# A two-layer graph-and-transformer kernel: five edits around the score table of the first layer

## The chip, the core and the metric

The kernel is one program on one core of a Trainium2 chip. The metric is the time of one execution in device microseconds, and the time of a kernel is the median of its runs. One more execution was taken with the profiler on; its times are those of the trace.

## What is computed

The reference takes 625 nodes with 1024 features and 10,000 directed edges. Layer 0 adds graph attention, linear attention and a ternary-weight feed-forward to the nodes; layer 1 adds a neighbour-mean network, a second linear attention and a mixture of experts. The part that the change touches is the graph attention of layer 0 and what runs beside it:

```python
msg = xl[src] + xr[dst]                       # per edge, 4 heads of 64
act = jnp.where(msg > 0, msg, 0.2 * msg)
e = jnp.einsum('ehd,hd->eh', act, att)        # one score per edge and head
alpha = softmax of e over the edges of one dst (self loops included)
out = segment_sum(alpha[..., None] * xl[src], dst) @ W_up
# beside it, from the same normed x:
k, v = phi(x @ W_k + b_k), x @ W_v + b_v      # 1024 columns, made in two halves of 512
# then, node by node:
x = x + graph part + mix part + b_o
x = x + ffn(layernorm(x));  xn1 = layernorm(x)   # quantised activations, ternary weights
```

## The kernel before, in words

Nodes lie in `NT = 5` tiles of `P = 125`. All weights are float32; a weight half of 1024 x 512 is loaded by `Half` as two transfers of 1 MB on SP's queue into a pool of six buffers with the tag "w".

**The order.** In this part the order of the work on each engine is the order in which the program emits it. `Stream` (called `do`) holds back the steps that follow a matmul group, so that a group's evacuation is emitted after the next call's preparation and before the next call's matmuls; an argument-less `do()` only lets held steps out. Each engine runs its own list in order.

**The edges.** `left_right` (L537) writes the left and right projections of each tile to DRAM, `xl_d` on ACT's queue and `xr_d` on POOL's. Then POOL issues, for each of 79 chunks of 128 edges, two gathers (L601, `ga` and `gb`) and one scatter (L619) of the finished scores into `table`, a DRAM array of 625 x 625 x 4 scores that a single transfer (L395) fills with zeros first. Between them DVE adds and reduces (`score_group`, L609 to L584) and ACT raises to e (L588). A scatter waits until the scatter before it has landed. `one_beat` issues one step of this chain; `work(us)` paces the beats by the matmul time that was emitted. Five of the beats also run `self_loops(t)`: the scores of the nodes' own loops, `own`, which ACT's queue stores onto the diagonal of `table` (L164 and L165 inside `rows_dma`, two transfers for one tile: partitions 0 to 111 and 112 to 124).

**The dense work beside it.** `lin.key(t)` and `lin.value(t)` make the keys and values of one half of the columns for all five tiles, with `count()` between them (edge counts, L458); `lin.half(1)` then loads the biases (`bk_t`, `bv_t`) and the two weight halves of the second half. Queries, answers and the output projection `mixed` follow.

**The table.** After the last scatter, `load_table(t)` brings the 125 destination columns of tile t, 5 x 500 values per partition, into `tb` by two transfers on POOL's queue. `weigh(t)` multiplies them by the edge counts, one DVE instruction (L828) for each of five source tiles s; `sums(t)` contracts the result (`pg`, head by head, over all s).

**The tile periods.** A loop over `p` staggers the five tiles. In period p: `sums(p)`, `turn_sums(p)`, `weigh(p + 1)`, `up_again(p)` (L891, its evacuation into x is L896) for the graph part, and for tile p - 1 the feed-forward made by `ffn`: `p1` (layernorm and quantise, DVE), `f1` (eight transposes `ptr`, L948, evacuated at L949), `f2` (`pgu`, then a tanh on ACT and a chain on DVE), `f3` (transposes `phT`, evacuated at L980), `f4` (`pdn`, added into x at L996). For tile p - 2: `p5` (layernorm, DVE) and `f5` (eight transposes L1011, copied to `xnT1` by ACT at L1012). A `spacer` is one key or value group of layer 1's linear attention, placed between these steps. The output bias is added to x by ten DVE instructions (L1068), two for each tile: tiles 0 and 1 in period 0, tiles 2, 3 and 4 in period 1. Narrow PSUM tiles (`ps1`) take turns in two banks, wide ones (`ps2`) in three double banks.

Of the kernel before, what the change touches and what calls it, by code (L numbers as in the profile page):

```python
# [14 lines left out]
ALU = mybir.AluOpType  # L15
# [5 lines left out]
NT = 5  # L21
P = 125
# [31 lines left out]
def attempt(ctx: ExitStack, tc: tile.TileContext, w: dict, out: bass.AP, shifted: bool):  # L54

    nc = tc.nc
# [85 lines left out]
    def nodes(t):  # L142
        return slice(t * P, (t + 1) * P)
# [18 lines left out]
    def rows_dma(eng, dst, src):  # L162

        eng.dma_start(out=dst[0:112], in_=src[0:112])  # L164
        eng.dma_start(out=dst[112:P], in_=src[112:P])  # L165
# [32 lines left out]
    wpool = graph.enter_context(tc.tile_pool(name="w", bufs=6))  # L198
# [9 lines left out]
    hold = {}  # L208
# [138 lines left out]
    with ExitStack() as st0:  # L347
# [5 lines left out]
        tview = table[0:N * N, :].rearrange("(u p d) h -> p u (d h)", u=NT, p=P)  # L353
        xnT = bigT("xnT")

        with ExitStack() as edges:
# [22 lines left out]
            def load_edges():  # L379
                for dst, name in ((si, "src"), (di, "dst")):  # L380
# [10 lines left out]
            lin = LinearAttention(xnT, ("L0_Wq", "L0_Wk", "L0_bk", "L0_Wv", "L0_bv"), w["L0_bq"],  # L391
                                  lambda us: work(us), nc.sync)
# [3 lines left out]
                              in_=none.unsqueeze(1).to_broadcast([128, 28, 440]))  # L396
# [177 lines left out]
            def score(dst, m, n, p):  # L574

                by_att = att[0:p].unsqueeze(1).to_broadcast([p, n, 256])
                if shifted:
                    nc.vector.scalar_tensor_tensor(m, m, 0.2, m, op0=ALU.mult, op1=ALU.max)
                    nc.vector.tensor_tensor(m, m, by_att, op=ALU.mult)
                else:  # L580
                    nc.vector.scalar_tensor_tensor(m, m, 0.0, by_att, op0=ALU.max, op1=ALU.mult)
                nc.vector.tensor_reduce(dst, m.rearrange("p t (h e) -> p t h e", h=4), AX.X, ALU.add)
                if not shifted:
                    nc.vector.tensor_scalar(dst, dst, LIMIT, None, op0=ALU.min)  # L584

            def exp(e):
                if not shifted:
                    nc.scalar.activation(e, e, AF.Exp)  # L588
# [35 lines left out]
            own = pool.tile([P, NT, 4], FP, name="own")  # L624
# [8 lines left out]
            diagonal = table[0:N * (N + 1), :].rearrange("(s d) h -> s d h", d=N + 1)[:, 0, :]  # L633

            def self_loops(t):


                m = pool.tile([P, 1, 256], FP, tag="xd", name="gs", bufs=1)
                nc.vector.tensor_tensor(m[:, 0, :], xlr[:, t, 0:256], xlr[:, t, 256:512], op=ALU.add)
                score(own[:, t:t + 1, :], m, 1, P)  # L640
                exp(own[:, t:t + 1, :])
                rows = xlr[:, t, 0:256].rearrange("p (h e) -> p h e", h=4)
                if shifted:
                    nc.vector.tensor_copy(xl1[:, t, :, 0:64], rows)
                else:
                    nc.vector.tensor_tensor(m[:, 0, :], xlr[:, t, 0:256], att[:P], op=ALU.mult)
                    nc.vector.tensor_reduce(linear[:, t, :], m.rearrange("p t (h e) -> p (t h) e", h=4), AX.X, ALU.add)
                    part4 = pool.tile([P, 4, 1], FP, tag="part4", name="part4", bufs=2)
                    nc.vector.tensor_scalar(part4[:, :, 0], linear[:, t, :], -4.0 * LINEAR, 4.0 * LINEAR,
                                            op0=ALU.max, op1=ALU.min)  # L650
                    nc.scalar.activation(xl1[:, t, :, 64:65], part4, AF.Exp, scale=0.25)
                    nc.vector.tensor_tensor(xl1[:, t, :, 0:64], rows,
                                            xl1[:, t, :, 64:65].to_broadcast([P, 4, 64]), op=ALU.mult)
                rows_dma(nc.scalar, diagonal[nodes(t), :], own[:, t, :])

# [32 lines left out]
            def work(us):  # L690
                beat["us"] += us

                while beat["us"] >= 2.0 + 5.2 * min(beat["g"], 6) + 8.1 * max(beat["g"] - 6, 0) and chunks:
                    one_beat()
# [2 lines left out]
            states = []  # L697
            for c in range(2):
                if c:
                    lin.half(c)  # L700
                for t in range(NT):
                    for f in (lin.key, lin.value):
                        f(t)
                        part["held"] = max(part["held"] - 1, 0)
                        for _ in range(6):
                            if count():
                                work(0.7)
                states.append(lin.states())
                if c == 0:
                    for f in states[0]:  # L710
                        f()
# [15 lines left out]
            def mixed(t, ks=range(KC), keep=None, then=None, paced=True, cs=(0, 1)):  # L727
                for c in cs:
                    def pe(c=c):
                        if c == 0 and ks[0] == 0:  # L730
                            hold["px", t] = ps2("px1")
                        for k in ks:
                            nc.tensor.matmul(hold["px", t][:P, c, :], lhsT=oT[:, k, nodes(t)], rhs=wo[c](k),  # L733
                                             start=(k == 0), stop=(k == KC - 1 and keep is not None))

                    def after():
                        px = hold.pop(("px", t))
                        for c in range(2):
                            nc.vector.tensor_tensor(keep[:, c, :], px[:P, c, :], bo[c][:P], op=ALU.add)  # L739

                    do(None, pe, after if keep is not None and c == 1 else None)
                    if then is not None and c == 0:
                        then()
                    if paced:
                        work(0.87 * len(ks))
# [29 lines left out]
            for m in range(KC):  # L775
# [5 lines left out]
                if m < 3:  # L781
# [3 lines left out]
                                      in_=w[("w_gate", "w_up", "w_down")[m]].rearrange("(k p) n -> p k n", p=128))  # L785
# [4 lines left out]
            bo = [lin.bias(w["L0_bo"], c, tag) for c, tag in enumerate(("bk_t", "bv_t"))]  # L790
# [4 lines left out]
            kept = mid([P, 2, 512], "kept")  # L795
# [14 lines left out]
        x = xpool.tile([P, NT, D], FP, name="x")  # L810
# [3 lines left out]
        def load_table(t):  # L814

            hold["tb", t] = mid([P, NT, P, 4], "tb")
            if not shifted:
                rows_dma(nc.gpsimd, hold["tb", t].rearrange("p s d h -> p s (d h)"),
                         tview[:, :, t * 4 * P:(t + 1) * 4 * P])

        def weigh(t):

# [203 lines left out]
        made_of = {}  # L1026

        def spacer():

            f, t = next(kv_pieces)  # L1030
            getattr(lin1, f)(t)

        for p in range(NT + 2):
            do()
            if p >= 2:
                made_of[p - 2][5]()
            if 1 <= p <= NT:
                made_of[p - 1] = ffn(p - 1)
                made_of[p - 1][0]()
            if p == 1:  # L1040
                mixed(4, cs=(0,))
            if p >= 3:
                spacer()
            if p >= 2:
                made_of[p - 2][6]()
            if p == 0:
                xnT1 = bigT("xnT1")
                nc.gpsimd.memset(xnT1[:, :, N:NP], 0.0)
                lin1 = LinearAttention(xnT1, ("L1_Wq", "L1_Wk", "L1_bk", "L1_Wv", "L1_bv"), w["L1_bq"],
                                       lambda us: None, nc.gpsimd)  # L1050
                lin1.large = True
            if p < NT:
                sums(p)
            if 1 <= p <= NT:
                made_of[p - 1][1]()
                do()
                made_of[p - 1][2]()
            do()
            if p < NT:
                turn_sums(p)  # L1060
            if p + 1 < NT:
                weigh(p + 1)
            if p + 2 < NT:
                load_table(p + 2)
            for t in ((0, 1), (2, 3, 4))[p] if p < 2 else ():
                for c in range(2):
                    xc = x[:, t, c * 512:(c + 1) * 512]
                    nc.vector.tensor_tensor(xc, xc, kept[:, c, :] if t == 3 else bo[c][:P], op=ALU.add)  # L1068
            if p == 1:
                mixed(4, cs=(1,))  # L1070
                lin1.weights(0)
                lin1.half(0, loaded=True)
            if 2 <= p <= NT:
                spacer()
            if 1 <= p <= NT:
                made_of[p - 1][3]()
            do()
            if p < NT:
                up_again(p)
            if 1 <= p <= NT:  # L1080
                made_of[p - 1][4]()
# [170 lines left out]
    for b in range(NB_MIN, NB):  # L1252
        nc.gpsimd.dma_start(out=y_d[b * 128:(b + 1) * 128, :].rearrange("p (a n) -> p a n", a=4),
                            in_=zero.unsqueeze(1).to_broadcast([128, 4, 256]))
# [452 lines left out]
    for i in range(3):  # L1707
        d = 1 << i
# [240 lines left out]
```

## Time and profile before

| what | value |
|---|---|
| median of 7 runs | 2197.57 us (2195.75 to 2204.39) |
| profiled execution, its own time | 2200.19 us |
| span of its trace | 2198.4 us |
| mean granted TensorE clock | 0.981 |
| TensorE matmul busy | 2108.2 us (96%) |
| VectorE busy | 712.1 us (32%) |
| GpSimd busy | 338.5 us (15%) |
| DMA moved | 301.62 MB, mean 137 GB/s |

PE is TensorE, DVE VectorE, ACT ScalarE, POOL GpSimd and SP the sync engine. An "idle before" is time in which an engine waited, and the name behind the arrow is what ended the wait. Times inside the trace are microseconds from the start of the span. The granted clock is 1.00 where TensorE ran at full rate.

### The profile page before, as it was taken

The numbers are of one execution on the slowest core, as the hardware profiler recorded it, in microseconds if no ns is written. First come the engines' busy times: TensorE is split into PE (matmuls) and PEld (weight loads), VectorE is DVE, ScalarE is ACT, GpSimd is POOL, SyncE is SP. The second block draws the span as 40 slices with busy tenths as digits, with TensorE's granted clock in tenths as the row PEclk, the third lists the DMA queues.
The fourth block names the chain that finished last, engine by engine and source line by source line (L and its number), as shares of the span: only waits on it lengthen the run. The fifth ranks groups of instructions, "written<-read, shape, count | busy, mean of one in ns | idle before, by whom it ended". The sixth has DMA issues, their size and how long they took to land. (4 is left out here: it accounts for less than half of the span.)

```text
span 2198.4 us, 17365 instructions
## 1 busy us (share of the span) xinstructions
PE 2108.2 (96%) x6934; PEld 1208.9 (55%) x6934; DVE 712.1 (32%) x1214; ACT 194.0 (9%) x354; POOL 338.5 (15%) x349
## 2 busy tenths in 40 slices
PE   7999999589899999999999999999999999999998
PEld 6665574355455687754446777457744444444443
DVE  5786486467432740000122143222111111111012
ACT  2000110012211100000000111100000000000000
POOL 1666677400000200210000000110000000000011
PEclk9999999679999999999999999999999999999999
DMA  9335432440122110150303101022099978997732
GB/s 300 86 108 172 145 112 85 109 128 11 39 86 77 48 39 28 59 182 0 104 11 106 61 16 39 29 95 96 31 362 343 330 290 311 329 329 282 278 140 90
DMA packets 145848, 301.62 MB, mean 137 GB/s; under 512 B 12370, under 2 KB 22436, under 8 KB 145754
## 3 DMA queue, kind: packets, MB, share of 16 engines
q1 hardware_dynamic: 123700, 244.23, 31.2%
q0 software_dynamic: 17376, 46.42, 7.2%
q10 hardware_dynamic: 4678, 9.72, 1.4%
q8 instruction: 58, 0.95, 0.2%
q14 instruction: 36, 0.29, 0.0%
HBM read 277.49 MB, written 22.84 MB: 137 GB/s over the span
## 5 line engine op out<-in xcount | busy, mean ns | idle before, releaser
L130 PE MATMUL pu<-w,xgT 128*128 128x512 f32 x768 | 333.9, 593 | 1.9 <-DVE xgT L1243 1.9
L130 PEld LDWEIGHTS pu<-w,xgT 128*128 128x128 f32 x768 | 144.0, 190 | 174.8 <-issue 172.0
L130 PE MATMUL pyb<-w,hb 128*128 128x512 f32 x384 | 174.3, 598 | 2.5 <-ACT yb L105 2.1
L130 PE MATMUL pk<-w,xnT 128*125 128x512 f32 x320 | 140.8, 593 | 1.7 <-DMA w<-in_L_Wk_dram 1.5
L130 PE MATMUL pv<-w,xnT 128*125 128x512 f32 x320 | 141.7, 596 | 0.1
L130 PE MATMUL pq<-xnT,w 128*128 128x313 f32 x512 | 138.1, 428 | 1.0 <-DVE v L277 0.8
L130 PE MATMUL p<-tT,w 128*128 128x313 f32 x512 | 136.3, 428 | 0.4 <-DVE tT L1243 0.4
L130 PEld LDWEIGHTS pyb<-w,hb 128*128 128x128 f32 x384 | 69.8, 189 | 90.9 <-issue 74.8
L130 PEld LDWEIGHTS pq<-xnT,w 128*128 128x128 f32 x512 | 97.3, 191 | 40.1 <-DVE v L277 1.6
L1783 DVE TENSOR_TENSOR su<-pu,su 128x512 f32<-128x512 f32 x24 | 16.6, 691 | 314.6 <-ACT su L1782 314.6
L130 PEld LDWEIGHTS p<-tT,w 128*128 128x128 f32 x512 | 96.8, 190 | 37.9 <-issue 1.2
L130 PEld LDWEIGHTS pv<-w,xnT 128*125 128x125 f32 x320 | 59.9, 189 | 73.5 <-issue 72.0
L130 PEld LDWEIGHTS pk<-w,xnT 128*125 128x125 f32 x320 | 59.5, 188 | 73.5 <-issue 72.5
L619 POOL DMA_INDIRECT table<-es,at x79 | 83.4, 1055 | 62.1 <-issue 25.6
L1766 POOL DMA_INDIRECT xg<-rows_d,slots x12 | 11.3, 943 | 524.8 <-PE pxg L1773 449.0
L601 POOL DMA_INDIRECT ga<-xl_d,si x79 | 80.5, 1019 | 33.8 <-issue 30.0
L601 POOL DMA_INDIRECT gb<-xr_d,di x79 | 79.2, 1003 | 24.1 <-issue 23.8
L733 PE MATMUL px<-w,oT 128*125 128x512 f32 x160 | 71.9, 608 | 6.6 <-DVE kept L739 5.2
L1132 DVE TENSOR_TENSOR z<-pz,z 125x512 fp32r<-125x512 f32 x10 | 6.9, 691 | 196.8 <-ACT z L1130 196.8
L130 PE MATMUL px<-w,hT 128*125 128x512 f32 x160 | 70.3, 592 | 0.0
L130 PE MATMUL px<-w,oT 128*125 128x512 f32 x160 | 70.3, 592 | 0.0
L130 PE MATMUL ph<-meanT,w 128*128 128x313 f32 x256 | 70.0, 426 | 0.0
(366 smaller groups left out, 2520.4 us busy)
## 6 DMA issues: line engine op xcount, KB each, us to landing
w<-in_eW_dram SPq DMA_DIRECT2D x144, 1024.0 KB
w<-in_L_Wk_dram SPq DMA_DIRECT2D x8, 1024.0 KB
w<-in_L_Wv_dram SPq DMA_DIRECT2D x8, 1024.0 KB
w<-in_L_Wq_dram SPq DMA_DIRECT2D x8, 1024.0 KB
w<-in_L_Wo_dram SPq DMA_DIRECT2D x8, 1024.0 KB
w<-in_W_self_dram SPq DMA_DIRECT2D x8, 1024.0 KB
w<-in_W_neigh_dram SPq DMA_DIRECT2D x8, 1024.0 KB
w<-in_sW_dram SPq DMA_DIRECT2D x8, 1024.0 KB
```

The costliest lines, as they stand in the source:

```text
L130: nc.tensor.matmul(dst, lhsT=lhsT, rhs=rhs, start=(i == 0), stop=(i == len(pairs) - 1))
L601: nc.gpsimd.indirect_dma_start(out=ab[g][side][0:p, j, :], out_offset=None, in_=src[:, :], in_offset=bass.IndirectOffsetOnAxis(ap=ix[0:p, ...
L619: nc.gpsimd.indirect_dma_start(out=table[:, :], out_offset=bass.IndirectOffsetOnAxis(ap=at[0:p, lo + j:lo + j + 1], axis=0), in_=es[0:p, l ...
L733: nc.tensor.matmul(hold["px", t][:P, c, :], lhsT=oT[:, k, nodes(t)], rhs=wo[c](k), start=(k == 0), stop=(k == KC - 1 and keep is not None))
L1132: nc.vector.tensor_tensor(low, src, high.bitcast(FP), op=ALU.subtract)
L1766: nc.gpsimd.indirect_dma_start(out=xg, out_offset=None, in_=rows_d[:, :], in_offset=bass.IndirectOffsetOnAxis(ap=slots[:, b:b + 1], axis=0))
L1783: nc.vector.tensor_tensor(su, pu[:, 0, :], su, op=ALU.mult)
```

## The change

Five edits, all in layer 0:

1. `self_loops` no longer stores `own` tile by tile. The last of the five stores all tiles at once (112 and 13 partitions, 5 x 4 values each).
2. The key weights of the second half (`wk1`) are asked for at tile 1 of the first half; the second half then loads its biases and its value weights only.
3. `load_table(0)` moves from POOL's queue to ACT's, in six transfers: partitions 112 to 124 whole, then partitions 0 to 111 for each source tile s. `load_table(1)` to `(4)` stay as they were.
4. The output bias of tiles 2 and 4 is added in period 2, behind `p1` of tile 1; that of tile 3 stays in period 1.
5. In the last period with a new feed-forward tile (p = 5), `p5` and `f5` of tile 3 no longer come first: `p5` runs after `f1` of tile 4, `f5` after `f2` of tile 4.

```diff
-                rows_dma(nc.scalar, diagonal[nodes(t), :], own[:, t, :])
+                if t == NT - 1:
+                    by_tile = diagonal.rearrange("(t p) h -> p t h", p=P)
+                    rows_dma(nc.scalar, by_tile, own)
...
                 if c:
-                    lin.half(c)
+                    lin.biases(c)
+                    lin.wk, lin.wv = wk1, Half(wpool, w["L0_Wv"], c)
+                    lin.half(c, loaded=True, biased=True)
                 for t in range(NT):
+                    if c == 0 and t == 1:
+                        wk1 = Half(wpool, w["L0_Wk"], 1)
...
-                rows_dma(nc.gpsimd, hold["tb", t].rearrange("p s d h -> p s (d h)"),
-                         tview[:, :, t * 4 * P:(t + 1) * 4 * P])
+                dst, src = hold["tb", t].rearrange("p s d h -> p s (d h)"), tview[:, :, t * 4 * P:(t + 1) * 4 * P]
+                if t == 0:
+                    nc.scalar.dma_start(out=dst[112:P], in_=src[112:P])
+                    for s in range(NT):
+                        nc.scalar.dma_start(out=dst[0:112, s, :], in_=src[0:112, s, :])
+                else:
+                    rows_dma(nc.gpsimd, dst, src)
...
+        def add_bias(*ts):
+            for t in ts:
+                for c in range(2):
+                    xc = x[:, t, c * 512:(c + 1) * 512]
+                    nc.vector.tensor_tensor(xc, xc, kept[:, c, :] if t == 3 else bo[c][:P], op=ALU.add)
+
         for p in range(NT + 2):
             do()
-            if p >= 2:
+            if p >= 2 and p != NT:
                 made_of[p - 2][5]()
             if 1 <= p <= NT:
                 made_of[p - 1] = ffn(p - 1)
                 made_of[p - 1][0]()
             if p == 1:
                 mixed(4, cs=(0,))
+            if p == 2:
+                add_bias(2, 4)
             if p >= 3:
                 spacer()
-            if p >= 2:
+            if p >= 2 and p != NT:
                 made_of[p - 2][6]()
...
             if 1 <= p <= NT:
                 made_of[p - 1][1]()
                 do()
+                if p == NT:
+                    made_of[p - 2][5]()
                 made_of[p - 1][2]()
+                if p == NT:
+                    made_of[p - 2][6]()
             do()
...
-            for t in ((0, 1), (2, 3, 4))[p] if p < 2 else ():
-                for c in range(2):
-                    xc = x[:, t, c * 512:(c + 1) * 512]
-                    nc.vector.tensor_tensor(xc, xc, kept[:, c, :] if t == 3 else bo[c][:P], op=ALU.add)
+            if p < 2:
+                add_bias(*((0, 1), (3,))[p])
```

## The prediction

> **What bounds the kernel now.** I read the page first: TensorE is busy for 2108.2 of 2198.4 us, so only some 90 us can be won without touching its work. Then TensorE's waits, sorted, and the wait behind the longest:
>
> ```profile
> PE pg L130 <- DVE pT L828: 25.2, 5, 24.1
> DVE pT L828 <- DMA tb<-table: 24.6, 1, 24.6
> ```
>
> The reader sees one stall of 24.1 us, before the first `pg`, passed on from `tb`. The timeline of POOL and DVE says what `tb` waited for:
>
> ```profile
> 410.36 0.85 POOL L619 DMA_INDIRECT table<-es,at  x1 [1.91 <-DMA table<-es,at]
> 412.97 0.90 POOL L164 DMA_DIRECT2D tb<-table  x1 [1.75 <-DMA table<-es,at]
> 421.95 4.83 DVE L828 TENSOR_TENSOR pT<-tb,CT 125x500 f32<-125x500 f32 x5 [24.61 <-DMA tb<-table]
> ```
>
> POOL's chain of gathers and scatters ends at 411; the table then takes 9 us to come and DVE 4.8 us to weigh. From 58 to 411 POOL steps about every 1.3 us with a gap of 0.30 us, so it is the bound of that stretch: time TensorE wins before 399 is lost in the stall unless POOL wins it too. POOL's real waits from 60 to 200 us:
>
> ```profile
> POOL table L619 <- DMA table<-own: 5.0, 3, 1.8
> POOL table L619 <- DMA table<-es,at: 4.3, 2, 2.8
> POOL table L619 <- ACT es L588: 2.4, 1, 2.4
> ```
>
> After 600 us TensorE is busy 1575.96 of 1590 us, so what is won or lost before then reaches the end unchanged.
>
> **1. Own scores stored once.** Three of the five stores each hold one scatter, for 1.67, 1.76 and 1.62 us by POOL's timeline; each would have been a 0.30 us gap. Two of these go: 1.37 + 1.46 = 2.8 us. The remaining store has five times the packets (16 bytes, 8 to 9 ns each in the DMA records, 35 instead of 7 for each engine): 0.3 us more. POOL wins 2.5 us (bounds 0.5, if the one store waits 2 us longer, and 2.8). The store still holds ACT, now earlier than its scatter lands; behind it are `es` exponentials that POOL needs only for later scatters. TensorE loses two waits on `ring` (2.23 and 0.78 us), which came from ACT standing at the third and fourth store while DVE waited for `kf`.
>
> **2. Key weights early.** Between 159 and 182 us the DMA engines are full (busy share 1.00 to 1.08) with 8 MB: keys, values, queries and two raw matrices. POOL's waits there are 4.10, 2.77, 2.38 and 1.52 us; without the usual 0.30 each, 9.6 us. With 2 of the 8 MB gone I take a quarter, 2.4 us (bounds 1, and 3.3 for the last two waits gone). TensorE also loses 1.46 us of waiting for the key weights. The 2 MB now go out behind the first half's value weights, about 55 to 60 us, when the last rows of `xl_d` are stored and the first gather (58.19) waits for them. SP passes nothing else: biases follow at 143. That store was issued at 52.88 and released the gather 5.0 us after its issue ended, in half-full queues. In the full stretch a scatter's successor came 6.3 us after it (164.53 to 170.81), so 1.3 us more is the near bound and 2 MB at 385 GB/s = 5.4 us the far one; I take half the near bound, 0.7 us. POOL's net on parts 1 and 2: 2.5 + 2.4 - 0.7 = 4.2 us (1 to 6). TensorE's 2.23 + 0.78 + 1.46 = 4.5 us let it keep: at 268.63 POOL waits 2.98 us for ACT's `qe`, which TensorE paces, so 4.5 is about the most that passes.
>
> **3. The table in pieces.** Now: whole table landed at 421.95, last piece weighed at 426.8. With pieces, DVE weighs while the others land; only the last needs its 1.05 us after landing: 3.8 us won if the landing stays. ACT issues at 0.31 to 0.42 us each (its stores of `own`), so six take 2.1 us and the last leaves at 415.1; ACT has nothing else until 435. Landing alone would be by 1.1 MB at 380 GB/s, 2.9 us, near 418.5; that would win 3.5 us more. But `x` of tile 0 (0.5 MB) and `tb` of tile 1 (1.2 MB), formerly queued behind, now leave POOL at the same moment: 2.9 MB in all at the 0.30 MB/us that the queue moved here is 9.8 us from 412.5, so the last piece could land as late as 422.3 or later. I take landing 0.2 us earlier than now and 4.0 us won in all (bounds -6 and +8). The next users stand clear: `weigh(1)` starts at 434.6 with its table already there.
>
> The Trainium skill (DMA: Bandwidth & Descriptors, Issuing engines are not separate DMA queues) states that transfers from different engines interleave on the same 16 DMA engines and that a second issuing engine saves little more than issue time; by that rule nothing of the landing is won and this part is 3.8 us or less.
>
> **4. The bias moved.** Period 1, on DVE:
>
> ```profile
> 467.67 0.69 DVE L1068 TENSOR_TENSOR x<-x,bk_t 125x512 f32<-125x512 f32 x1
> 468.87 1.30 DVE L1068 TENSOR_TENSOR x<-x,kept 125x512 f32<-125x512 f32 x2
> 470.67 0.69 DVE L1068 TENSOR_TENSOR x<-x,bv_t 125x512 f32<-125x512 f32 x1
> 471.60 1.22 DVE L896 TENSOR_TENSOR x<-px,x 125x1024 f32<-125x1024 f32 x1
> 472.88 1.86 PE L130 MATMUL pdn<-dn,room 128*125 128x512 bf16 x4 [3.42 <-DVE x L896]
> 478.79 1.93 PE L1011 MATMUL ptr<-ident,xn 125*128 125x125 f32 x8 [4.04 <-DVE xn L1003]
> ```
>
> Six additions stand before L896, and `pdn` waits for L896 to free its bank. Four go: 4 x 0.60 = 2.4 us. L896 cannot start before L891's matmuls end at 469.46, so it starts at 469.6 instead of 471.6: 2.0 us. `pdn` then runs at full clock, 1.08 (as at 505.25) instead of 1.86: 0.6 us net at L996. So 2.6 us at `f5`. In period 2 the four additions stand behind `p1` (ends 484.4) and before `dens` (490.18), 5.8 us idle: covered, and if `pg` there ran at full clock they would be last by some 2 us. The layer-1 bias loads on POOL now wait for these additions, with `load_table(4)` behind them; it was issued at 490.45, after them, so nothing is lost. Bounds: 1.5; and 6.5 if the clock stays up, since `pg` took 8.66 us here and 4.5 elsewhere.
>
> **5. The last period.** Now: `f5` at 569.62, then
>
> ```profile
> 573.33 1.04 PE L948 MATMUL ptr<-ident,room 125*128 125x125 f32 x8 [2.69 <-DVE room L925]
> 574.72 3.63 PE L130 MATMUL pgu<-gu,room 128*125 128x512 bf16 x8 [0.35 <-DVE room L949]
> 578.15 7.06 PE L130 MATMUL pk<-w,xnT 128*125 128x512 f32 x16
> 575.64 1.28 ACT L965 ACT_TABLE_LOAD   x1 [4.33 <-DVE rgu L964]
> ```
>
> After: DVE starts `p1` at 564.86 and ends at 570.2; `f1` 570.3 to 571.3; evacuation to 572.2; `pgu` 571.7 to 573.7. But `p5` (3.0 us) now stands on DVE ahead of the `rgu` pair, so these end at 575.55, and the table load that waits for them, the tanh and L966 to L968 end at 578.5. The order of the built kernel shows that `f5`'s second four transposes take the bank of `pgu`, which L968 reads last. So TensorE does four transposes at 574.8, stands 3.3 us, does four at 578.6 and starts `pk` at 579.1: 0.95 us later than now. A gap of 2.69 us here was followed by half clock from 574.7 to 578.1, so I expect the 3.3 us gap to cost up to 1.9 us in `pk` as well, and put 1.45 on it. Loss 2.4 us (0.9 to 3.3).
>
> The skill (TensorE: Matmul & The Clock Gate, Part 1) gives the full clock back after one busy window of about 3.4 us; by that the cost of a gap is at most 1.7 us. The rows here say more where the work is thin: the windows view has granted clock 0.50 for all of 472.3 to 492.7, while TensorE was busy for 14.82 us of it. In part 5 dense `pk` follows, so rule and row part little; in part 4 the row decides, and I leave the half clock in period 2 as it is.
>
> **Sum.** 4.2 + 4.0 + 2.6 - 2.4 = 8.4 us. The profiled execution, 2200.19 (span 2198.4), would become 2191.8 (span 2190.0); it lies 2.6 above the median, and from 2197.6 the forecast is **2189.2**.
>
> **Rivals.**
> (a) *The stall re-forms*: POOL's waits return elsewhere (another scatter or `es` is late), parts 1 and 2 give nothing. For: POOL waits 22.1 us on scatters over the whole stretch, mostly behind transfers that stay. Against: the lost waits have named causes. Then 4.2 less: 2193.4.
> (b) *ACT's queue starves*, the one that ends slower: at 414 to 431 us POOL's packets of the table are 6000 bytes in the DMA records, ACT's would be 2000. If each DMA engine takes one of each in turn, ACT gets a quarter of 0.30 MB/us while POOL's loads of `x` and `tb` go on, and 1.2 MB last 16 us: last piece weighed near 433 instead of 426.8, 6 us lost instead of 4 won: 2199.2, and 2203.4 with (a) too. It decides once the last piece lands after 430; before that the other parts still win. Against: POOL's 3.7 MB run out of turn whenever it waits, as it does at 421 and 429.
> (c) *The clock stays up in period 2*, and the pieces land by 418.5: 4 + 3.5 more, 2181.7.
> (d) *Parts 3 to 5 only shift work*: pieces 0, part 5 at its worst, 4.2 + 0 + 1.5 - 3.3 = 2.4: 2195.2.
>
> **How the numbers follow.** A measurement of this kernel can tell about 0.2%, 4.4 us, from no change. Chances: forecast 0.44, (a) 0.17, (b) 0.13, (c) 0.13, (d) 0.13. Low ends all together (POOL 1, pieces 0, 1.5, -3.3) give 2198.4, high ends (6 + 8 + 6.5 - 0.9) 2178; the range is 2180 to 2200, which leaves out part of (b) and the edge of (c). Faster by over 0.2% (below 2193.2) are the forecast, (c) and half of (a): 0.66; (d), the rest of (a) and part of (b) are within: 0.23; slower 0.11.
>
> **What would show it.** Right: last scatter issued near 406; `tb` pieces on ACT's queue with L828 as five separate starts about a microsecond apart; the wait of `pg` under 21 us; the wait of `pdn` on x near 1.4; a wait of about 3.3 us of `ptr` or `pk` between `pgu` and `pk` of the last period. Wrong: a first gather after 60, a last scatter still at 411, L828 ending after 426, or a half-clock stretch that grew.

## The result and the profile after

The changed kernel took 2201.85 us in the median (2196.9 to 2206.43), the kernel before 2200.9 beside it: a ratio of 1.0005, with a 95% interval of 0.9999 to 1.0011. Nothing was won. The profiled execution has a span of 2202.3 us, 3.9 more than before, and a mean granted clock of 0.979. Single executions of one kernel lie up to 5 to 7 us from their median, so a pair of spans shows where time moved, and the ratios say how much.

Three waits of the changed kernel, what they waited for, with total, number and longest; the first two answer to the stall shown of before (25.2 and 24.6 us):

```profile
PE pg L130 <- DVE pT L839: 32.8, 5, 23.4
DVE pT L839 <- DMA tb<-table: 29.8, 5, 21.9
POOL table L619 <- DMA table<-own: 1.9, 1, 1.9
```

The stall grew by 7.6 us, although one wait on `own` is left of three. The timeline of POOL, ACT and DVE says how:

```profile
408.46 0.85 POOL L619 DMA_INDIRECT table<-es,at  x1 [1.91 <-DMA table<-es,at]
409.31 0.59 POOL L164 DMA_DIRECT2D x<-in_x_dram  x1
410.97 0.87 POOL L164 DMA_DIRECT2D tb<-table  x1 [0.51 <-issue]
410.77 2.51 ACTq L828 DMA_DIRECT2D tb<-table  x5
417.30 1.04 DVE L839 TENSOR_TENSOR pT<-tb,CT 125x500 f32<-125x500 f32 x1 [21.87 <-DMA tb<-table]
420.63 1.04 DVE L839 TENSOR_TENSOR pT<-tb,CT 125x500 f32<-125x500 f32 x1 [2.29 <-DMA tb<-table]
423.86 1.04 DVE L839 TENSOR_TENSOR pT<-tb,CT 125x500 f32<-125x500 f32 x1 [2.18 <-DMA tb<-table]
426.64 1.04 DVE L839 TENSOR_TENSOR pT<-tb,CT 125x500 f32<-125x500 f32 x1 [1.75 <-DMA tb<-table]
429.44 1.03 DVE L839 TENSOR_TENSOR pT<-tb,CT 125x500 f32<-125x500 f32 x1 [1.75 <-DMA tb<-table]
```

The last scatter starts 1.9 us earlier than before (410.36). From there on I count from it and call its start S. POOL sends `x` and `tb` of tile 1 at once, and ACT's pieces come about 3 us apart instead of one: the first is weighed at S + 8.8, the last is done at S + 22.0. Before, the whole table had come at S + 11.6 and was weighed at S + 16.4. So the pieces cost 5.6 us where 4.0 were to be won. From 409 to 430 us POOL's queue moved 3.37 MB beside the 1.25 MB of the pieces.

The transfers by queue in a window of 416 to 420 us (queue, kind: packets, MB, share of the engines' time):

```profile
q0 software_dynamic: 146, 0.84, 81.2%
q10 hardware_dynamic: 130, 0.23, 23.7%
```

q0 is POOL's queue, q10 ACT's. Each moved nearly as many packets, but POOL's are 6000 bytes in the records and ACT's 2000, so ACT got 0.23 of 1.07 MB. (The counts take in a few records of 4 bytes; without these and other short ones they are 142 and 115.)

The other two places, in the timeline of TensorE. Most lines of before that answer to them stand in the prediction; that of the `pgu` of period 2 is:

```profile
492.02 2.31 PE L130 MATMUL pgu<-gu,room 128*125 128x512 bf16 x8
```

The changed kernel:

```profile
474.67 1.02 PE L130 MATMUL pdn<-dn,room 128*125 128x512 bf16 x4 [1.31 <-DVE x L907]
479.74 1.93 PE L1022 MATMUL ptr<-ident,xn 125*128 125x125 f32 x8 [4.05 <-DVE xn L1014]
492.98 3.62 PE L130 MATMUL pgu<-gu,room 128*125 128x512 bf16 x8
...
574.15 1.94 PE L130 MATMUL pgu<-gu,room 128*125 128x512 bf16 x8 [0.35 <-DVE room L960]
577.37 0.62 PE L1022 MATMUL ptr<-ident,xn 125*128 125x125 f32 x4 [1.28 <-DVE xn L1014]
580.39 1.09 PE L1022 MATMUL ptr<-ident,xn 125*128 125x125 f32 x4 [2.40 <-DVE rgu L978]
581.28 9.25 PE L130 MATMUL pk<-w,xnT 128*125 128x512 f32 x16
593.68 1.08 PE L130 MATMUL pdn<-dn,room 128*125 128x512 bf16 x4 [2.95 <-DVE room L991]
594.60 7.03 PE L130 MATMUL pv<-w,xnT 128*125 128x512 f32 x16
```

`pdn` waits 1.31 us for x instead of 3.42: part 4 does what was forecast. In the last period `f5` stands ahead of its first four transposes and again ahead of its second, for 1.28 and 2.40 us, and `pk` takes 9.25 us instead of 7.06. By stages: the last scatter -1.9, the table +5.6, part 4 -2.9 from the output projection (443.80 and 447.69) to `f5`, then +1.5 because `pgu` and `pgoT` of period 2 ran at half clock (3.62 us instead of 2.31), the last period +1.1: 3.4 of the 3.9 us.

### The profile page after: what moved, and what is told of

Same layout as the page of the kernel before. It is cut to its first block, busy times and chain, and to the rows that moved or that the text cites. A ratio compares the mean times of both kernels' runs of the same rounds, so it can differ in the third digit from the quotient of the medians.

```text
span 2202.3 us, 17357 instructions
## 1 busy us (share of the span) xinstructions
PE 2108.8 (96%) x6934; PEld 1210.6 (55%) x6934; DVE 712.9 (32%) x1214; ACT 194.1 (9%) x354; POOL 340.0 (15%) x347
```

## The experiments

Two sets, e1 to e4 and e5 to e8, ran at a level where every kernel, the one before too (2267.22 and 2265.6 us), lost some 65 us ahead of 470 us; there only the ratio to the kernel before beside it and distances from S are used. The other runs and the first traces are at 2200 us. e3, e9 and e10 were executed once, so they give a trace and no ratio.

**The table stage.** Theory: the pieces lose to POOL's larger packets beside them. Rivals: six small transfers are slow by themselves, or their number is.

e1, x and tile 1 behind the pieces on ACT's queue:

```diff
-                    rows_dma(nc.gpsimd, dst, src)
+                    rows_dma(nc.scalar if t == 1 else nc.gpsimd, dst, src)
...
-            rows_dma(nc.gpsimd, x[:, t, :], xrows[t])
+            rows_dma(nc.scalar, x[:, t, :], xrows[t])
```

> All five edits stay; the loads of x (all tiles) and of the table columns of tile 1 move from POOL's queue to ACT's, behind the six pieces, so that nothing else moves while the pieces come. S is the start of the last scatter. In the changed kernel the last piece was weighed at S + 22.0 us (before the change: S + 16.4). Theory 'share' (ACT's 2000 byte packets lose to POOL's 4096 and 6000 byte ones): the pieces come at twice the rate or more, last piece weighed at S + 11 to S + 14, span 8 to 11 us shorter, near 2193. Rival 'slow by itself' (small packets, or six transfers, cost what they cost, 75 KB/us): S + 20 to S + 23, span unchanged.

Measured: first piece weighed at S + 5.8, DVE then runs all five without a wait, done at S + 10.65. Ratio 0.9965 (0.995 to 0.998). The rival falls: the same six transfers are fast when nothing runs beside them.

e2, the pieces on POOL's queue:

```diff
-                    nc.scalar.dma_start(out=dst[112:P], in_=src[112:P])
+                    nc.gpsimd.dma_start(out=dst[112:P], in_=src[112:P])
...
-                        nc.scalar.dma_start(out=dst[0:112, s, :], in_=src[0:112, s, :])
+                        nc.gpsimd.dma_start(out=dst[0:112, s, :], in_=src[0:112, s, :])
```

> All five edits stay, the six pieces go out on POOL's queue, ahead of x and of tile 1, which stay there. Theory 'share': in one queue the pieces are served before what is queued behind them; six issues at 0.6 to 0.9 us are done at S + 6, the last piece is weighed at S + 12 to S + 15. Rival 'slow by itself': S + 20 or later again. Rival 'queue': x and tile 1 in the same queue still run beside the pieces, S + 16 to S + 18.

Measured: done at S + 11.6, slightly better than the theory's lower end; ratio 0.9973 (0.9957 to 0.9988). In one queue the pieces, asked for first, were not held up by `x` and tile 1 behind them.

e3, whole on ACT's queue, and e4, whole on POOL's as before the change:

```diff
-                    nc.scalar.dma_start(out=dst[112:P], in_=src[112:P])
-                    for s in range(NT):
-                        nc.scalar.dma_start(out=dst[0:112, s, :], in_=src[0:112, s, :])
+                    rows_dma(nc.scalar, dst, src)      # e3
+                    rows_dma(nc.gpsimd, dst, src)      # e4
```

> All five edits stay, but the table of tile 0 goes out on ACT's queue whole, in two transfers as before, with x and tile 1 on POOL's beside it. Theory 'share': still late, landed near S + 20, last weighed near S + 25, as DVE starts only then; span 2 to 4 us longer than the changed kernel's. Rival 'piece count' (six transfers cost the time): landed at S + 11.6 and weighed at S + 16.4 as before the change, span 5 us shorter.

> The third edit alone is undone: table of tile 0 whole, on POOL's queue, first. By the reading of the two traces the edit cost 5.6 us: last piece weighed at S + 16.4, S at 408.5 again, span near 2196.7, ratio to the kernel before 0.998 to 0.9995. If instead the loss came from somewhere else that only shows there (the DVE or the clock): S + 18 or later and span within 2 us of 2202.

Measured for e3: landed and first weighed at S + 13.3, done at S + 18.1. My expectation (S + 25) was wrong. Its two issues were out by S + 2.8, where the pieces' were out by S + 4.8 in the changed kernel. By the records 509 of its 625 packets had started before POOL's first 6000 byte packet came, at S + 7.8; the last ones, beside those, crept at 50 KB/us. In the changed kernel that packet came at S + 5.5, when 102 of the 625 had started. This fits a price that depends on how much is left when the other stream starts. The six issues, spread over 2.9 us, left more; why POOL's packets also came 2.3 us later in e3, the runs do not show. e4: S + 15.8, ratio 0.9993 (0.9979 to 1.0007).

e6, the changed kernel as control:

> The changed kernel itself, as the control of this set on this chip. Last piece weighed at S + 20 to S + 23 (S: start of the last scatter; 22.0 in the first trace). Ratio to the kernel before 0.999 to 1.002. If the pieces come by S + 16 here, the loss in the first trace belonged to that chip or that execution.

Measured: done at S + 20.8, ratio 1.0029 (1.0009 to 1.0050); it repeats the first trace. Here it was slower than the kernel before by more than could be seen in the first comparison.

e9, x and tile 1 beside the pieces from SP's queue, and e10, x alone beside them from POOL's:

```diff
-                    rows_dma(nc.gpsimd, dst, src)
+                    rows_dma(nc.sync if t == 1 else nc.gpsimd, dst, src)    # e9, with x on nc.sync too
+                    rows_dma(nc.scalar if t == 1 else nc.gpsimd, dst, src)  # e10
```

> All five edits, but x and the table of tile 1 go out on SP's queue at the same time as ACT's six pieces, so that the same bytes move beside the pieces, from another hardware queue. Theory 'one packet each in turn': SP's packets should be 2000 bytes for tile 1 and 4096 for x; the pieces get a third beside x and half beside tile 1; last piece weighed at S + 13 to S + 17 (S + 20.8 and 22.0 with POOL's 6000 byte packets, S + 10.7 with nothing beside). Rival 'any traffic beside': the bytes beside decide, S + 20 to S + 22. Rival 'POOL's queue goes first': S + 10 to S + 12.

> All five edits, but only the table of tile 1 moves behind the pieces on ACT's queue; x stays on POOL's, beside them. Theory 'one packet each in turn': beside 4096 byte packets the pieces get a third, some 90 KB/us; with 1.25 MB to bring that is 10 to 13 us where x lasts that long (2.5 MB at 180 KB/us does); last piece weighed at S + 14 to S + 18. Rival 'tile 1 alone is in the way' (same table in DRAM): S + 10 to S + 12.

Measured: e9 done at S + 17.7, just over its range; e10 at S + 20.9, well over. In e9 tile 1 comes in 2000 byte packets too, and from 416 to 420 us SP's queue moved 276 packets and 0.57 MB, ACT's 238 and 0.44. e10 from 416 to 428 us:

```profile
q0 software_dynamic: 598, 1.92, 64.2%
q10 hardware_dynamic: 643, 1.14, 39.0%
```

Equal numbers again: beside 4096 byte packets ACT got 1.14 of 3.06 MB. So in three mixes and windows the two queues moved packets in numbers within a fifth of each other. It is not so in every stretch: from 414 to 416 us SP's queue moved 246 packets and ACT's 15 in e9, POOL's 27 and ACT's 150 in the changed kernel; what gave one queue the lead there is open. Tile 1's 6000 byte packets are not needed for the loss: x, which lasts longer than the pieces, costs as much by itself.

e11 is the kernel before with the third edit alone in e1's form; e12 has the fourth edit too.

```diff
-                rows_dma(nc.gpsimd, hold["tb", t]...)         # e11: load_table as changed,
+                    rows_dma(nc.scalar if t == 1 else nc.gpsimd, dst, src)
-            rows_dma(nc.gpsimd, x[:, t, :], xrows[t])
+            rows_dma(nc.scalar, x[:, t, :], xrows[t])
...
-            for t in ((0, 1), (2, 3, 4))[p] if p < 2 else (): # e12 in addition
+            if p < 2:
+                add_bias(*((0, 1), (3,))[p])                  # and add_bias(2, 4) at p == 2
```

> The kernel before with the third edit alone, in the form without POOL's traffic beside it (six pieces on ACT's queue, x and tile 1 behind them). If the other four edits give little, this is as fast as all five with the same form (ratio 0.9965 there): last piece weighed at S + 10.7 instead of S + 15.6, 5 us, ratio 0.9965 to 0.998. If the other edits carry the 4 us that the prediction gave them, 0.998 to 0.9985 here.

> As the run with the table alone, and the fourth edit (bias of tiles 2 and 4 in period 2). From the other traces the fourth edit brings pdn of tile 0 2 us forward and pk of tile 0 1.6 us, and less behind it: 1 to 2 us to the end, ratio 0.996 to 0.9975. Rival 'given back': the half clock of period 2 takes all of it, and the end is where the run with the table alone has it.

Measured: e11 done at S + 10.7, ratio 0.9977 (0.9963 to 0.9991); e12 0.9957 (0.9943 to 0.9972).

**The other parts.** The first and the second edit alone, on the kernel before:

```diff
-                rows_dma(nc.scalar, diagonal[nodes(t), :], own[:, t, :])   # e7
+                if t == NT - 1:
+                    rows_dma(nc.scalar, by_tile, own)
...
-                    lin.half(c)                                            # e8
+                    lin.wk, lin.wv = wk1, Half(wpool, w["L0_Wv"], c)
...
+                    if c == 0 and t == 1:
+                        wk1 = Half(wpool, w["L0_Wk"], 1)
```

> The kernel before with the first edit alone: one store of all own scores. The prediction gave it 2.5 us of POOL's time (bounds 0.5 and 2.8), and all of it to the end. If POOL's waits come back elsewhere (the rival), S is within 1 us of the kernel before (410.4) and so is the time. Where the chip is quiet: theory 2195 to 2198, rival 2199 to 2201; ratio 0.9988 against 1.000.

> The kernel before with the second edit alone: key weights of the second half asked for in the first. The prediction gave it 2.4 us of the burst less 0.7 us of a late first gather, net 1.7 (bounds 0 and 3). From the first trace of the changed kernel the first gather is not late (58.1) and POOL's waits between 140 and 180 us fell from 9.6 to about 8.2 us, so 1.4 us: S at 408.5 to 409. Rival: the waits only move to the raw matrices behind (260 to 300 us), S at 410 or later, ratio 1.000.

Measured: 1.0016 (0.9996 to 1.0035) and 0.9992 (0.9972 to 1.0012). Neither wins what can be seen, and the first interval leaves out the 0.9988 that was expected. At this level POOL also waits for DVE (8.15 us before one gather of e6), so these two runs do not price the POOL term at 2200 us, and a place of S cannot be compared with the first traces there.

e5 and e13 are one kernel, e1 without the fifth edit; e14 has only the first of the first two edits, e15 only the second; e16 is e1's kernel. Against e1:

```diff
-            if p >= 2 and p != NT:                    # e5, e13, e14, e15
+            if p >= 2:
...
-                if p == NT:
-                    made_of[p - 2][5]()               # and [6] likewise
...
-                    if c == 0 and t == 1:             # e14 in addition
-                        wk1 = Half(wpool, w["L0_Wk"], 1)
...
-                if t == NT - 1:                       # e15 in addition
-                    rows_dma(nc.scalar, by_tile, own)
+                rows_dma(nc.scalar, diagonal[nodes(t), :], own[:, t, :])
```

> The run with x and tile 1 behind the pieces on ACT's queue, and part 5 undone (p5 and f5 of tile 3 come first again in the last period). Theory 'part 5 costs': from the two first traces, pk of the last period took 9.25 us instead of 7.06 because TensorE stood for xn and rgu just before it; the whole part cost 1 to 2.4 us net. So from pdn of period 4 to the pk of the last spacer this run should be 1 to 2.5 us shorter than the changed kernel, and the ratio to the kernel before 0.994 to 0.997 where the chip is quiet. Rival 'part 5 pays': the stall of 3 to 4 us in front of f5 (4.04 before) comes back and the stretch is 1 us or more longer.

> Table in the form without traffic beside it, bias moved, own store once and keys early, the last period as before the change. S is the start of the last scatter. S was 408.5, 409.0 and 410.6 in three quiet traces with the first two edits and 410.4, 411.6 and 412.4 in three without: 2.1 us on average. Theory 'the POOL term is 2 us, not 4.2, and reaches the end': 2 us below the run with table and bias alone (2191.9, ratio 0.9957), so near 2190, ratio 0.9945 to 0.9955. Rival 'it is lost': as that run, ratio 0.9955 to 0.9965. Rival 'the full 4.2': 0.9935 to 0.994.

> The run with table and bias, and the single store of own scores. The prediction gave the store 2.5 us; the scatters of the first two traces show two of five waits gone and the rest 1.91 long, so 1.4 us by the sixth scatter. Theory 'most of what the two edits win is the store': ratio 0.0005 to 0.001 below the run with table and bias. Rival: the waits move, no difference.

> The run with table and bias, and the key weights asked for early. The prediction gave it 2.4 us less 0.7. POOL's waits in the burst fell only from 9.6 to 8.2 us in the changed kernel. Theory 'small': S 0 to 1 us earlier, no difference at the end that can be measured. Rival 'as predicted': 1.7 us, 0.0008 below the run with table and bias. Rival 'it costs': first gather after 59 and S later.

> All five edits, table in the form without traffic beside it; differs from the run without part 5 by the order of the last period alone. Theory 'part 5 costs 1 to 2.4 us on a quiet chip' (from L902 of tile 0 to the end 1762.7, 1760.6 and 1759.8 with it against 1758.7 without): ratio 0.0005 to 0.0011 above the run without part 5; pk of the last period 8 to 9 us long instead of 7.0. Rival 'no price' (0.06 us between the two in the slower set): the same ratio.

Measured: e5 0.9978 (0.9958 to 0.9998), where 0.994 to 0.997 was expected; e13 0.9954 (0.9941 to 0.9968), e14 0.9957 (0.9940 to 0.9975), e15 0.9955 (0.9938 to 0.9971), e16 0.9946 (0.9930 to 0.9961). The times of e12 to e16 do not tell these five apart. The traces do better for S: 407.4 in e13 and 407.3 in e16, with both edits; 412.0 and 412.7 with one alone.

e16 is the best ratio of all, 11.9 us below the kernel before (8.6 to 15.4). Its timeline, of ACT, DVE and TensorE, answers to that of the changed kernel:

```profile
409.61 2.27 ACTq L828 DMA_DIRECT2D tb<-table  x5
413.01 4.84 DVE L839 TENSOR_TENSOR pT<-tb,CT 125x500 f32<-125x500 f32 x5 [18.74 <-DMA tb<-table]
414.11 0.68 PE L130 MATMUL pg<-xl,pT 125*125 125x65 f32 x2 [20.46 <-DVE pT L839]
```

Before the change the last of these lines was:

```profile
423.05 0.68 PE L130 MATMUL pg<-xl,pT 125*125 125x65 f32 x2 [24.10 <-DVE pT L828]
```

The five pieces are weighed in one run, and the wait of `pg` ends 9 us earlier. Its transfers from 412 to 415 us:

```profile
q10 hardware_dynamic: 462, 0.81, 104.0%
```

ACT's queue alone moves 0.81 MB in 3 us, 270 KB/us, with the same small packets that made 58 KB/us beside POOL's.

**Parts 5 and 4 alone**, on the kernel before:

```diff
-            if p >= 2:                                # e17, twice
+            if p >= 2 and p != NT:
...
+                if p == NT:
+                    made_of[p - 2][5]()               # behind f1, and [6] behind f2
...
-            for t in ((0, 1), (2, 3, 4))[p] if p < 2 else ():   # e18
+            if p < 2:
+                add_bias(*((0, 1), (3,))[p])          # and add_bias(2, 4) at p == 2
```

> The kernel before with the fifth edit alone. From L891 (up_again) of tile 0 to the end of the span it took 1762.4 us before; with the fourth edit 1755.99 to 1758.73 in four traces, with fourth and fifth 1759.78 to 1762.66 in four. Theory 'it costs', as in the prediction (0.9 to 3.3 us): 1763.3 to 1766, ratio 1.0004 to 1.0015, pk of the last period long or split. Rival 'free': 1761 to 1762.5 and a ratio of 1.000 or below, as the comparison of times of the last set (0.9946 with it, 0.9954 without) would have it.

> The kernel before with the fourth edit alone. The prediction gave it 2.6 us (bounds 1.5 and 6.5). Theory 'it wins 2.6 to 4 us and keeps them to the end': L891 of tile 0 to the end 1758 to 1760, ratio 0.998 to 0.999. Rival 'given back in period 2, whose half clock grows': 1761 to 1762.5, ratio 0.9993 to 1.000.

Measured: e17 1.0010 (1.0000 to 1.0020), and 1765.0 us from L891 of tile 0 to the end, 2.6 more than before. Its TensorE in the last period:

```profile
578.14 0.62 PE L1011 MATMUL ptr<-ident,xn 125*128 125x125 f32 x4 [1.28 <-DVE xn L1003]
581.15 1.10 PE L1011 MATMUL ptr<-ident,xn 125*128 125x125 f32 x4 [2.40 <-DVE rgu L967]
582.04 9.24 PE L130 MATMUL pk<-w,xnT 128*125 128x512 f32 x16
```

These are the two waits and the slow `pk` of the changed kernel, to the hundredth: the last period is theirs, whatever happens at the table. e18: 0.9981 (0.9970 to 0.9993), 4.2 us won (1.5 to 6.6); its trace shows only 0.5 us of that from L891 to the end (1762.0), so the ratio speaks for the theory and the one trace for the rival.

## Why the prediction was wrong

The step that failed is in part 3: "I take landing 0.2 us earlier than now and 4.0 us won in all (bounds -6 and +8)". Measured, from S: -5.6 us. That is 9.6 of the 12.3 us between the forecast gain of 8.4 and the loss of 3.9 in the traces. Two things failed in it. It took the pieces to be among the first bytes that move, without a row that said so: they shared with POOL's loads, and the last was weighed at S + 22.0. And it counted 2.9 MB at 0.30 MB/us, with `x` of one tile only: POOL had issued `x` of four tiles and tile 1 by 415.7 us, before it first waited, and what moved from 409 to 430 us was 4.62 MB at 0.22 MB/us (the kernel before moved 223 GB/s from 414 to 431 us). Rival (b) had the mechanism, the packet sizes and nearly the price (a quarter of the rate, 6 us lost, last piece weighed near 433; measured 0.23 of 1.07 MB, 5.6 us, 430.5), and got 0.13. The argument against it, that POOL's loads run out of turn at its waits, did not bear, since they were issued before its first wait.

Two choices around the step matter too. The forecast of 2189.2 was counted from 2197.6, the median of seven runs; beside the changed kernel the same kernel had 2200.9, so 3.3 us of the miss are the base, and (b) counted from there is 2202.5. And the low end of the range took the pieces at 0, although their own bound was -6; with that bound it would have been 2204.4.

The gain itself was there, and larger than forecast: with nothing beside the pieces, the matmuls of `up_again` of tile 0 (L902 in the changed kernel) start 19.7 to 20.0 us after S in e11 to e16, against 24.8 to 25.6 in three traces with the table whole (before, e17, e18). That is 5 us, and e11 shows 5.1 us (2.0 to 8.1).

The Trainium skill (DMA: Bandwidth & Descriptors, Queues, rings and completion order) states that a DMA engine takes the queues with work in turn, a whole packet from each. The nearly equal packet numbers in the three windows above agree; the stretch from 414 to 416 us does not. The same page (Issuing engines are not separate DMA queues), cited in the prediction, says that a second issuing engine saves little; e1 and e6, two ways to issue the same bytes, differ by 10 us from S to the last weighing.

**POOL, 4.2 us.** Measured 1.9 us in the pair; S averages 408.6 in five traces with both edits (408.46, 409.04, 410.64, 407.44, 407.29) and 411.7 in five with neither (410.36, 412.38, 411.61, 412.98, 411.01): 3.1 us. The same ten traces show where it came and went. With both edits the first scatter starts 0.2 us earlier on average, the eighth, behind the own scores, 2.7 us (122.9 against 125.6), the twentieth, at the end of the burst, 4.3 us (179.5 against 183.8). So the store gave its 2.5 us and the burst 1.6 of the 2.4, and 1.2 us were lost again before S. The scatters of before and then of after, from 58 to 412 us (count | busy us, mean ns | idle before):

```profile
L619 POOL DMA_INDIRECT table<-es,at x79 | 83.4, 1055 | 62.1 <-issue 25.6 <-DMA table<-es,at 22.1 <-ACT es L588 5.2
```

```profile
L619 POOL DMA_INDIRECT table<-es,at x79 | 84.1, 1065 | 56.9 <-issue 29.1 <-DMA table<-es,at 23.0 <-DMA table<-own 1.9
```

In this pair the waits fell by 5.2 us, but the indirect DMAs with their gathers are 2.7 us longer in all (245.8 instead of 243.1), and the gathers' waits grew by 0.6. In the burst POOL's waits beyond 0.30 fell from 9.6 to 8.2 us; waits on the scatter before came back behind it (22.1 and 23.0 in all), as chance (a) had it in part. The first gather was not late (58.08), so the 0.7 us put there was not paid. e14 and e15, one trace each, show the early S with both edits only, and the two groups of five touch (410.64 with both, 410.36 with neither). In e14 the eighth scatter is early too (123.3), but not the last; why S needs both, the runs do not say.

**Part 4, 2.6 us.** 2.9 in the pair, of which half clock in period 2 took 1.5 back: the half-rate stretch was 20.5 us long in both traces, but began at 476.5 instead of 472.4 us, while the work came only 0.95 us later. Alone it gave 4.2 us (1.5 to 6.6), within the stated bounds.

**Part 5, -2.4 us.** -2.2 (-4.4 to 0) alone in time, -2.6 in its trace. The order of waits was as forecast: 3.7 us in `f5` where 3.3 were expected, and 2.2 us of half clock in `pk` where 1.45 were put. That a gap costs at most 1.7 us did not hold: the half-rate stretch around the two waits lasted 6.83 us (578.9 to 585.7), and `pk` alone lost 2.2. Later `pdn` and `pv`, now at full clock (593.68 and 594.60 above), give 1.7 us back, which the sum did not have; before they read:

```profile
588.37 1.94 PE L130 MATMUL pdn<-dn,room 128*125 128x512 bf16 x4 [2.95 <-DVE room L980]
590.11 7.90 PE L130 MATMUL pv<-w,xnT 128*125 128x512 f32 x16
```

Half rate was granted for 6.8 us of the last period in both kernels, before in two stretches of 3.41 us. Between e13 and e16 the times show no loss (0.9954 and 0.9946, each to 0.0014); the comparison of two edited kernels was too coarse for it.

Without the failed term the other parts sum to 4.2 + 2.6 - 2.4 = 4.4 us; e4, which has just these, shows 1.6 us (-1.6 to 4.8), too wide to settle it. Chance (d), that parts 3 to 5 only shift work, was nearly true of parts 4 and 5 in the pair (1.4 us won, 1.1 lost).

## What to carry to other kernels

When a transfer moves to another queue, ask what was waiting behind it in the old one: order within a queue was its priority (last piece weighed at S + 11.6 in e2), and that is lost (20.8 in e6). Beside a stream with larger packets the transfer here got about its packet's share of the bandwidth, not half (0.23 of 1.07 MB, 1.14 of 3.06), so put the urgent bytes and their followers on one queue, urgent first. Price each edit alone where times can't part two edited kernels: part 5 cost about 2 us (0 to 4.4) and hid beside gains.

## What had not been expected

That the share goes by packets came out nearer than I thought: 146 to 130, 598 to 643 and 276 to 238 packets in three mixes. The level of e1 to e8 was another surprise. From 75 to 100 us TensorE was busy for 8.67 of 25 us in e1 (25.00 in the changed kernel's first trace), between matmuls of `pct` that started 0.7 to 2.8 us apart and, by the profile, waited for nothing. The same kernels ran at 2200 us in other sets, and two chips showed both levels; what caused it stays open.

The clock's half-rate stretches in all records are multiples of 3.41 us (3.4, 6.8, 20.5, 47.8), apart from the one that the end of each record cuts off. The Trainium skill (TensorE: Matmul & The Clock Gate, Part 1) gives a free-running window of that length and calls its phase variable from run to run, which fits that the same periods cost 1756.0 to 1758.7 us in e12 to e15.
